# Where the statistics' tiny TensorE products sit: moved to other pairs of a conv-preact kernel

## The chip, the cores and the metric

The kernel runs on one core of a Trainium2 chip. The metric is the device time of one execution in microseconds (us), and the time of a kernel is the median of several runs. All arithmetic is float32.

## The reference, cut to what matters

The input x is 4 x 128 x 96 x 96 (batch, channels, rows, columns). Each batch is group-normalised over 32 groups of 4 channels, scanned in four directions by a small state-space block, fused and added to x:

```python
def _gn(v, G=32, eps=1e-5):
    g = v.reshape(B_, G, C_ // G, H_, W_)
    m = jnp.mean(g, axis=(2, 3, 4), keepdims=True)
    s = jnp.var(g, axis=(2, 3, 4), keepdims=True)
    return ((g - m) / jnp.sqrt(s + eps)).reshape(v.shape)
...
t = _grouped1x1(x, in_proj_w, in_proj_b, G)          # x is _gn(x) in one of four orders
u, gate = (t[:, :HID], t[:, HID:])
u = depthwise_conv5(silu(u))
...                                                  # s, a, bb, cc from u; scan along the sequence
u = u + _conv1x1(cc * hst + ssm_d[None, :, None] * s, ssm_out_w)
u = _grouped1x1(u * jax.nn.sigmoid(gate), mix_w, mix_b, G)
return _conv1x1(u, out_proj_w, out_proj_b)
...
x = x + fuse(four directions)
```

The kernel never normalises x. It scales the in_proj weights by 1/sqrt(variance) and puts the mean into the bias. For each batch it therefore needs, before that batch's first in_proj, the group means and variances, a scaled weight tile `wn` and a bias tile `bnorm`.

## The kernel before, in words

**Units and pairs.** There are 8 phases: for each of 4 batches one V phase (the two column directions) and one H phase (the two row directions). A phase has 24 pairs, so a batch has 48 pairs and the program 192 (`NU // 2`). `pair(t)` (L777) writes out the instructions of one pair by hand. The order of instructions on each engine is exactly the order of the code, because the whole body stands under a manual schedule. Below, "pair 38" means the pair with t % 48 = 38 of a batch: 0 to 23 are the V phase, 24 to 47 the H phase.

**What one pair issues on TensorE** (the lines are those of the profile; most products are recorded under the helper `mm`, L134): `conv` (`sil,band`), `accumulate` (`u,w_fin`, the output product of a unit six pairs back), `conv_less` (`sil,less`), `gate` (L491) and `out_of` (L497), and last `proj` (`u,main`, 32 loads and 32 matmuls). Pairs differ in three things:

- Pairs with t % 24 in 20 to 23 or 0 to 7 also compute in_proj (`x_in,wn` through L134) for the pair four ahead (`with_front`).
- Pairs with t % 24 in 6 to 17 compute gates (`gate`, L491). The other pairs read stored gates (`old`).
- So in the H half of a batch: pairs 24 to 29 have in_proj, 30 and 31 in_proj and gates, 32 to 41 gates alone, 42 and 43 neither, 44 to 47 in_proj.

TensorE uses three shapes of weight tile here: 128*32 and 64*32 (columns in four groups; `u,w_fin`, `u,main`, `sil,band`, the statistics, and `sil,less`), and 32*128 (gates and `out_of`). In_proj is 32*32.

**PSUM banks.** There are eight. Banks 0 to 3 take `out_of`; banks 0 and 1 also hold the running sum of the conv taps, which VectorE builds (L630). `PROJ` is (4, 5), `FRONT` is (7, 6, 2, 3). A pair takes its conv and proj banks and its accumulate banks `w` from `plan` (L125). In pairs 42 and 43 conv goes to banks 7 and 6, accumulate to 4 and 5, and proj to 4 and 5 at the end. With in_proj and fresh gates, the first gate goes to bank 6; with gates alone, to bank 4 (`GATE`, L123).

**The statistics of the next batch.** During the V phase VectorE takes chunk statistics of the next batch (`bn_stats`). At the end of pair 23 a generator `stats_finish(b + 1)` (L180) is made, and `stats_piece` (L818) advances it by one piece in every pair with t % 4 > 1. It has eight pieces:

1. `bn_aggr` on VectorE (`mv`).
2. Mean product: 4 matmuls `mv,gmean` (8 loads, a one-column right side) into bank `free[0]`; VectorE copies `mean` (L193), then `dev` (L195), `ex` (L197), `gm` (L199).
3. Variance product: 8 matmuls `ex,gmean` (16 loads); VectorE `var` (L207) and two integer steps on `inv`; GpSimd first Newton turn (4 tiny operations, L223 to L226).
4. and 5. Second and third Newton turn on GpSimd.
6. VectorE: two scalings that make `wn` (L230).
7. First bias product: 4 matmuls `gm,wn`; VectorE `bnorm` (L246), `shift` (L249), `spread` (L250).
8. Second bias product: 4 matmuls `spread,id`; VectorE `bnorm` (L255, L256).

Before the change the pieces fall in pairs 26, 27, 30, 31, 34, 35, 38, 39. Only three batches have a next batch: the last batch has none of these pieces.

**The bank of a tiny product** is `free[0]`. In pairs without in_proj, or with stored gates, it is `w[0]` (bank 7 in pair 27, bank 4 in pairs 38 and 39), straight after `accumulate` into `w[0]` and `w[1]`. In pairs 30 and 31 it is `w[1]`, bank 6, straight after `conv_less`.

**Around the end of a pair.** ScalarE copies finished conv sums out of PSUM into `us` (L609, or L611 for banks 6 and 7 in one instruction), copies `u` into the out_of banks (`under`, L505), and copies accumulate results to `ys` (L737). GpSimd adds `ys` to `acc` (L754). VectorE gates the finished unit (L577) and adds the taps of the next pair (L630); the last tap writes `us`, which `u,main` reads.

Of the kernel before, what the change touches and what calls it, by code (L numbers as in the profile page):

```python
# [63 lines left out]
NP = NS * R  # L64
# [3 lines left out]
def conv_preact_kernel(  # L68
# [53 lines left out]
    FRONT = (7, 6, 2, 3)  # L122
    GATE = {True: (6, 4, 5, 7), False: (4, 7, 6, 5)}  # L123

    def plan(with_front):  # L125

        return (PROJ, FRONT[:2]) if with_front else (FRONT[:2], PROJ)

    def bank(i):
        return psum[:, i, :]  # L130

    def mm(o, col, lhsT, rhs, start, stop):
        r = slice(32 * col, 32 * col + 32)
        nc.tensor.matmul(o[r, : rhs.shape[-1]], lhsT, rhs, start=start, stop=stop,  # L134
                         skip_group_check=True)
# [33 lines left out]
    stats, free = {}, [FRONT[1]]  # L169
# [92 lines left out]
    def fresh(step):  # L262

        return step * UB < NU and step % NS < NS // 2
# [11 lines left out]
    def mirror(n):  # L276

        return None if n % NP < NP // 2 else NP - 1 - n % NP
# [128 lines left out]
    def front_parts(i, banks, half=False):  # L407

        step, g = divmod(i, R)
        if step * UB >= NU:  # L410
            return
        st = step % NS
        if st == NS // 2:
            sils[step] = sils[step - 1]
            load_silu(step + 1, (g,))
        elif st == NS - 1 and g < 2:
            load_silu(step, (2 * g, 2 * g + 1))
        elif g == 0 and fresh(step):
            sils[step] = wk.tile([P, 2, 2, 4, N + 1], F32, tag="sil", name=f"sil_{step}")
        if fresh(step):  # L420
            yield from compute_front(step, g, banks, half)
        if st == 0:
            for j in range(2):
                edges(step, g, j, nc.gpsimd)
        after_front(step, g)
# [216 lines left out]
    def proj(i, banks, apart=False):  # L642

        step, p = units[i]["step"], units[i]["p"]
        if step not in scans:
            t0 = wk.tile([P, N, R], F32, tag="t0", name=f"t0_{step}")
            scans[step] = t0.rearrange("p n r -> p r n")
        ta = scans[step]
        tb = tbs[i] = wk.tile([P, N], F32, tag="t1", bufs=LAG + 1, name=f"t1_{units[i]['id']}")

        turns = [(e, j) for j in ((1, 0) if i else (0, 1)) for e in range(2)]
        apart = apart or not i
        for e, j in sorted(turns) if apart and i else turns:
            if i == 0 and (e, j) == (0, 0):
                first = front_parts(R, (5, 4, 2, 3), half=True)
                next(first)
                next(first)
                first_tap(2)
                for _ in first:
                    pass  # L660
            for c, cols in enumerate(((qb, qb, qa, qa), (qs, qs, qc, qc))[e]):
                first, end = (j == 0, j == 1) if apart else (j == 1, j == 0)
                mm(bank(banks[e]), c, w_proj[:, j, cols], us[i][:, c % 2, j, :], first, end)
        pa, pb = (bank(bk)[:, :N] for bk in banks)

        tm = tms[i] = wk.tile([P, N], F32, tag="tm", name=f"tm_{units[i]['id']}")
        nc.scalar.activation(tm, pa, AF.Tanh, bias=b_proj[:, 0:1])  # L667
        nc.scalar.copy(tb[0:64, :], pb[0:64, :])
        if i == NU - 2:
            nc.scalar.activation(  # L670
                ta[64:P, p, :], tm[64:P, :], AF.Identity, bias=mid[64:P, :], scale=HALF
            )
        nc.scalar.activation(tb[64:P, :], pb[64:P, :], AF.Tanh, bias=b_proj[64:P, 1:2])  # L673
        if i < NU - 2:
            nc.gpsimd.tensor_scalar(*decay(i))  # L675
        nc.gpsimd.tensor_mul(ta[0:64, p, :], tb[0:64, :], tm[0:64, :])  # L676

    def decay(i):

        a = scans[units[i]["step"]][64:P, units[i]["p"], :]  # L680
        return (a, tms[i][64:P, :], HALF, MID, ALU.mult, ALU.add)
# [5 lines left out]
    def first_tap(i):  # L687
        if i < NU:
            taps(i, range(1))
# [16 lines left out]
    def outputs(i, copy=nc.gpsimd.tensor_copy, engine=nc.gpsimd):  # L706
        ta, tb, p = scans[units[i]["step"]], tbs[i], units[i]["p"]
        engine.tensor_mul(ta[0:64, p, :], tb[64:P, :], ta[64:P, p, :])  # L708
        engine.tensor_add(tb[0:64, :], ta[0:64, p, :], tb[0:64, :])  # L709
        if copy:  # L710
            copy(tb[64:P, :], tb[0:64, :])  # L711
# [50 lines left out]
    later, soon = [], []  # L762
# [14 lines left out]
    def pair(t):  # L777
        i, k, bi = 2 * t, t % R, 2 * (t - LAG)
        back = bi >= 0
        old = back and mirror(bi // 2) is not None  # L780

        late = bi > 2 and (bi - 2) % (NU // B) == 0
        with_front = fresh((t + R) // R)
        final = (nc.vector, True) if t == NU // 2 - 1 else ()
        seed = old or back and not with_front

        ahead = old or back and not with_front
        banks, w = plan(with_front or not back)
        if not back:
            banks = head_banks(t)  # L790
        if back:
            front(t + R, FRONT)
        for n in soon:
            load_kept(n)
        soon.clear()
        if seed and not with_front:
            under(bi, 1)
        if t < NU // 2 - 2:
            send()

        if len(reload) == 4 and (k == 1 or late):
            for b, r in reload:
                nc.sync.dma_start(accf[:, r], xr[b, :, r])
            reload.clear()
        if t:
            new_u(i)
            taps(i, range(1, K))
            conv(i, banks)
        if t and not ahead:
            conv_less(i, banks)  # L810
        if not back and t:
            first_tap(i + 2)
            front(t + R, FRONT if banks == PROJ else (5, 4, 2, 3))
        recurrence(t)
        un = units[i]
        stats_chunks(t)

        def stats_piece():  # L818
            if later and k > 1:
                next(later[0], None)  # L820

        if not ahead:
            free[0] = w[1]
            stats_piece()
        if seed and with_front:
            for s in (1, 0):
                under(bi, s)
        for add in held:
            add()
        held.clear()  # L830
        if waiting:
            add = accumulate(waiting.pop(0), w[0], *final)
            if late:
                held.append(add)
            else:
                add()

        between = ahead and not old
        if between:
            conv_less(i, banks)  # L840
        if seed and not with_front:
            under(bi, 0)
        if ahead:
            accumulate(waiting.pop(0), w[1], *final)()
            free[0] = w[0]
            stats_piece()
            if not between:
                conv_less(i, banks)
        if old:
            scale_s(i - 2)  # L850
            for s in range(2):
                for j in range(2):
                    out_of(bi, s, j)
                load_gate(bi + s + UB)
        elif back:
            gates_and_out(bi, with_front)
        if back:
            for s in range(2):
                gating(bi, s)
        if un["order"] == "V" and un["b"] + 1 < B and un["st"] == NS - 1 and k == R - 1:  # L860
            later[:] = [stats_finish(un["b"] + 1)]
        if t + 2 < NU // 2:
            load_chunks(t + 2)
        if back:

            if k == 2 and t + 1 < NU // 2:
                soon.append(bi // 2 + 2)
            else:
                load_kept(bi // 2 + 2)
            if waiting:  # L870
                add = accumulate(waiting.pop(0), w[1])
                if late:
                    held.append(add)
                else:
                    add()
            first_tap(i + 2)
        if t == NU // 2 - 1:
            for s in range(2):
                under(bi + 2, s)
        if t == NU // 2 - 1:  # L880
            outputs(i - 8, None)
        proj(i, PROJ if back else banks, between)
        if not old and t > 0:
            scale_s(i - 2)
        if back:
            waiting.extend(units[bi : bi + 2])
        if t >= NU // 2 - 4:
            load_last(t)

        if bi > 0 and bi % (NU // B) == 0:  # L890
            send()
# [281 lines left out]
```

## Time and profile before

| what | value |
|---|---|
| median of 3 runs | 1819.84 us (1818.55 to 1820.01) |
| profiled execution, its own time | 1821.96 us |
| its span, first to last instruction | 1820.2 us |
| granted TensorE clock, mean | 0.998 |
| busy: PE, ACT, DVE, POOL | 98%, 86%, 80%, 78% |

How long single pairs take is read from the timeline of TensorE's weight loads: from the first load of one pair's `u,main` group to the first load of the next pair's. In us, for the pairs in question and for the same pairs of the last batch, which carry no statistics:

| pair of the batch | batch 0 | batch 1 | batch 2 | batch 3 |
|---|---|---|---|---|
| 26 | 9.265 | 9.264 | 9.264 | 9.264 |
| 27 | 9.822 | 9.816 | 9.816 | 9.264 |
| 28 | 9.328 | 9.384 | 9.384 | 9.327 |
| 30 | 9.954 | 9.954 | 9.955 | 9.828 |
| 31 | 10.178 | 10.181 | 10.180 | 10.182 |
| 34 | 9.110 | 9.110 | 9.110 | 9.110 |
| 35 | 9.111 | 9.111 | 9.111 | 9.111 |
| 38 | 9.690 | 9.689 | 9.690 | 9.109 |
| 39 | 9.624 | 9.621 | 9.622 | 9.111 |
| 42 | 8.410 | 8.407 | 8.408 | 8.408 |
| 43 | 8.251 | 8.251 | 8.250 | 8.251 |

A pair of one kind repeats to a few nanoseconds, so the rows can be compared directly. PE is TensorE's matmuls, PEld its weight loads, DVE VectorE, ACT ScalarE, POOL GpSimd. Matmul ends are modelled, so starts of loads are the firmer marks.

### The profile page before, as it was taken

What the parts mean: (1) busy time and instruction counts of PE and PEld (TensorE: products, weight loads), DVE (VectorE), ACT (ScalarE), POOL (GpSimd) and SP (SyncE); (2) the same over time, 40 slices, a digit from 0 to 9 for tenths busy, and PEclk for the clock granted to TensorE, in tenths of its full rate; (3) what the DMA queues carried; (4) which work ended last, traced back from release to release, by engine and by line L of the source; (5) the groups of instructions that cost most, each with busy time, mean ns of one, the idle gap of its engine ahead of it and who ended that gap; (6) DMA issues with size and microseconds to landing.
All of it is one profiled execution on the core that took longest, in us unless ns stands there. A gap on an engine that the chain in (4) does not pass through costs nothing.

```text
span 1820.2 us, 56934 instructions
## 1 busy us (share of the span) xinstructions
PE 1792.3 (98%) x24074; PEld 645.5 (35%) x24074; DVE 1454.6 (80%) x1462; ACT 1562.5 (86%) x2748; POOL 1428.2 (78%) x1475
## 2 busy tenths in 40 slices
PE   6999999999999999999999999999999999999998
PEld 3333333333333333333333333333333333333333
DVE  6888878877888888877778888887877788778885
ACT  4888888988988888888888888888888888888974
POOL 3587878778778888788877888887877888887785
PEclk9999999999999999999999999999999999999999
DMA  8555463444975465334696456453477644635434
GB/s 246 175 190 179 149 203 99 162 142 154 313 242 181 158 196 171 119 135 137 224 296 227 141 179 210 119 171 110 161 237 223 227 148 129 197 102 177 149 125 155
DMA packets 148047, 321.17 MB, mean 176 GB/s; under 512 B 14160, under 2 KB 115920, under 8 KB 147792
## 3 DMA queue, kind: packets, MB, share of 16 engines
q1 hardware_dynamic: 147648, 317.48, 54.2%
q8 instruction: 190, 3.11, 0.7%
q14 instruction: 65, 0.53, 0.1%
q10 hardware_dynamic: 144, 0.04, 0.0%
HBM read 185.21 MB, written 132.25 MB: 174 GB/s over the span
## 4 chain that ended last, share of the span: by engine, by line
PE 94%; ACT 2%; DVE 2%; DMA 1%; issue 0%; SPq 0%; POOL 0%; DVEq 0%; ACTq 0%; POOLq 0%
PE psum L134 81%; PE psum L497 8%; PE psum L491 5%; DMA xs<-in_xr 1%; ACT psum L505 1%; ACT sil L470 1%; DVE psum L630 1%; DMA acc<-in_xr 0%; DVE bn L298 0%; ACT u L611 0%; DVE u L577 0%; DVE u L630 0%; ACT psum L628 0%; DVE t L702 0%; SPq L296 0%
## 5 line engine op out<-in xcount | busy, mean ns | idle before, releaser
L630 DVE SCALAR_TENSOR_TENSOR psum<-sil,small,psum 128x768 f32<-128x768 f32 x576 | 589.0, 1023 | 28.8 <-ACT psum L628 3.4
L134 PE MATMUL psum<-u,w_fin 128*32 128x384 f32 x6176 | 553.1, 488 | 0.2 <-ACT t L673 0.2
L577 DVE SCALAR_TENSOR_TENSOR u<-gate,psum 128x768 f32<-128x768 f32 x376 | 349.8, 952 | 249.0 <-ACT gate L514 107.2
L134 PE MATMUL psum<-u,main 128*32 128x384 f32 x6144 | 534.9, 489 | 1.6 <-DVE u L630 1.5
L754 POOL TENSOR_TENSOR acc<-ys,acc 128x384 f32<-128x384 f32 x374 | 410.7, 1120 | 32.1 <-ACT ys L735 10.8
L708 POOL TENSOR_TENSOR t<-t,t 64x384 f32<-64x384 f32 x191 | 232.3, 1216 | 153.8 <-DVE t L702 70.2
L134 PEld LDWEIGHTS psum<-u,w_fin 128*32 128x32 f32 x6176 | 188.9, 110 | 322.4 <-issue 216.6
L134 PEld LDWEIGHTS psum<-u,main 128*32 128x32 f32 x6144 | 181.9, 109 | 328.4 <-issue 200.7
L505 ACT COPY psum<-u 128x768 f32<-128x768 f32 x352 | 276.7, 799 | 23.1 <-DVE u L630 11.3
L134 PE MATMUL psum<-sil,band 128*32 128x384 f32 x3072 | 285.2, 488 | 0.0
L675 POOL TENSOR_SCALAR t<-tm 64x384 f32<-64x384 f32 x191 | 177.2, 928 | 123.2 <-ACT tm L667 104.2
L709 POOL TENSOR_TENSOR t<-t,t 64x384 f32<-64x384 f32 x191 | 246.8, 1292 | 15.0
L497 PE MATMUL psum<-t,main 32*128 32x384 f32 x1536 | 242.1, 514 | 3.3 <-ACT psum L505 2.6
L628 ACT ACTIVATE psum<-sil,small 128x768 f32<-128x768 f32 x191 | 173.2, 907 | 61.1 <-DVE u L577 52.8
L514 ACT ACTIVATE gate<-psum,bnorm 128x384 f32<-128x384 f32 x384 | 192.1, 582 | 30.1 <-PE psum L491 28.6
L676 POOL TENSOR_TENSOR t<-t,tm 64x384 f32<-64x384 f32 x192 | 195.1, 1016 | 15.3
L630 DVE SCALAR_TENSOR_TENSOR u<-sil,small,psum 128x768 f32<-128x768 f32 x192 | 194.9, 1015 | 7.8
L470 ACT ACTIVATE sil<-psum,bnorm 128x385 f32<-128x385 f32 x384 | 192.1, 585 | 3.7 <-PE psum L134 1.5
L134 PE MATMUL psum<-sil,less 64*32 64x384 f32 x3072 | 168.1, 495 | 0.0
L491 PE MATMUL psum<-x_in,wn 32*128 32x384 f32 x768 | 157.4, 526 | 3.0 <-DVE shift L249 1.4
L711 POOL COPY t<-t 64x384 f32<-64x384 f32 x188 | 141.2, 751 | 15.5 <-PE psum L134 3.6
L134 PEld LDWEIGHTS psum<-sil,band 128*32 128x32 f32 x3072 | 90.3, 109 | 169.6 <-issue 94.4
(102 smaller groups left out, 1484.3 us busy)
## 6 DMA issues: line engine op xcount, KB each, us to landing
sil<-sil SPq DMA_DIRECT2D x128, 770.0 KB, 6.8
kept<-gate SPq DMA_DIRECT2D x80, 768.0 KB, 3.7
gate<-kept SPq DMA_DIRECT2D x76, 768.0 KB, 5.1
x_in<-in_xs SPq DMA_DIRECT2D x192, 96.2 KB, 2.5
out<-acc SPq DMA_DIRECT2D x48, 384.0 KB, 8.0
acc<-in_xr SPq DMA_DIRECT2D x39, 384.0 KB, 6.9
xs<-in_xr SPq DMA_DIRECT2D x72, 192.0 KB, 5.5
x_in<-in_xs SPq DMA_DIRECT2D x46, 192.5 KB, 3.5
```

Of the source, the lines that this page charges most:

```text
L134: nc.tensor.matmul(o[r, : rhs.shape[-1]], lhsT, rhs, start=start, stop=stop, skip_group_check=True)
L470: nc.scalar.activation(sils[step][:, s, j, g, :], bank(bk)[:, : N + 1], AF.Silu, bias=bn[:, 1:2] if j else bn[:, 4 + g : 5 + g],)
L491: nc.tensor.matmul(bank(to)[:, :N], stats[un["b"]][0][r, s, :], x_in[s][r, q, off : off + N], start=True, stop=True)
L497: nc.tensor.matmul(bank(SSM + 2 * s + j)[:, :N], w_so[r, bass.ts(j, P)], z[r, :], start=bi not in seeded, stop=True, skip_group_check=True)
L505: nc.scalar.copy(psum[:, SSM + 2 * s : SSM + 2 * s + 2, :N], us[bi][:, s])
L514: nc.scalar.activation(gv[:, s, j, :], bank(to[2 * s + j])[:, :N], AF.Tanh, bias=bn[:, 2 + j : 3 + j], scale=0.5,)
L577: nc.vector.scalar_tensor_tensor(v, g, 1.0, pz, ALU.add, ALU.mult)
L630: nc.vector.scalar_tensor_tensor(us[i][:, :, 1, :] if k == K - 1 else part, src, w_tap[:, k : k + 1], part, ALU.mult, ALU.add,)
L676: nc.gpsimd.tensor_mul(ta[0:64, p, :], tb[0:64, :], tm[0:64, :])
L708: engine.tensor_mul(ta[0:64, p, :], tb[64:P, :], ta[64:P, p, :])
L709: engine.tensor_add(tb[0:64, :], ta[0:64, p, :], tb[0:64, :])
L754: adder.tensor_add(part, y, part)
```

## The change

`stats_piece` gets a flag and a place. Pairs 27 and 39 no longer advance the generator. In pairs 42 to 47 (`ending`: stored gates, second half of the H phase) the usual call does nothing, and a second call stands after `out_of`, the gating and the loads, just ahead of `proj`, with bank 7 (`FRONT[0]`) as the product's bank. The eight pieces fall in pairs 26, 30, 31, 34, 35, 38, 42, 43. So the mean product is in pair 30 and the variance product in pair 31, both in the place where the variance product of pair 30 was; the Newton turns are in 31, 34 and 35; `wn` is made in 38; and the two bias products are in pairs 42 and 43, between `out_of` and `u,main`. The first batch's statistics, at the start of the program, and all other instructions keep their order.

```diff
@@ -815,8 +815,10 @@
         un = units[i]
         stats_chunks(t)
 
-        def stats_piece():
-            if later and k > 1:
+        ending = old and t % (2 * NP) > NP + NP // 2
+
+        def stats_piece(at_end=False):
+            if later and k > 1 and at_end == ending and t % (2 * NP) not in (27, 39):
                 next(later[0], None)
 
         if not ahead:
@@ -879,6 +881,9 @@
                 under(bi + 2, s)
         if t == NU // 2 - 1:
             outputs(i - 8, None)
+        if ending:
+            free[0] = FRONT[0]
+            stats_piece(True)
         proj(i, PROJ if back else banks, between)
         if not old and t > 0:
             scale_s(i - 2)
```

## The prediction

> **What bounds the kernel now.** I read the page first, then who waited for whom on TensorE, then the timeline around each tiny product.
>
> ```profile
> span 1820.2 us, 56934 instructions
> PE 1792.3 (98%) x24074; PEld 645.5 (35%) x24074; DVE 1454.6 (80%) x1462; ACT 1562.5 (86%) x2748; POOL 1428.2 (78%) x1475
> ...
> PE 94%; ACT 2%; DVE 2%; DMA 1%; issue 0%; SPq 0%; POOL 0%; DVEq 0%; ACTq 0%; POOLq 0%
> ```
>
> TensorE is the bound everywhere: 98% busy, and 94% of the chain that ended last. So an edit is worth what it does to the distance between TensorE's loads. Who waited on PE names the products at once:
>
> ```profile
> PE psum L491 <- DVE shift L249: 1.4, 3, 0.5
> PE psum L491 <- DVE bnorm L255: 1.2, 3, 0.4
> PE psum L134 <- ACT ys L737: 0.9, 3, 0.3
> ```
>
> Each is 3 times, once per batch that has a next one. But an idle time of PE is not the cost; the pair's length is. Loads of `u,main`, pair 38 of batch 0 and of batch 3 (no statistics):
>
> ```profile
> 362.76 0.16 PEld L134 LDWEIGHTS psum<-u,main 128*32 128x32 f32 x8 [0.57 <-ACT gate L514]
> 372.45 0.16 PEld L134 LDWEIGHTS psum<-u,main 128*32 128x32 f32 x8 [0.62 <-ACT gate L514]
> ...
> 1693.06 0.16 PEld L134 LDWEIGHTS psum<-u,main 128*32 128x32 f32 x8 [0.57 <-ACT gate L514]
> 1702.17 0.16 PEld L134 LDWEIGHTS psum<-u,main 128*32 128x32 f32 x8 [0.57 <-ACT gate L514]
> ```
>
> 9.69 against 9.11: the first bias product costs 0.58 us. The last batch is a control for every pair, and the table of pair lengths above gives the rest. The end of pair 38 shows why:
>
> ```profile
> 369.53 0.13 PEld L134 LDWEIGHTS psum<-u,w_fin 128*32 128x32 f32 x4 [0.19 <-issue]
> 369.85 0.13 PEld L134 LDWEIGHTS psum<-gm,wn 128*32 128x32 f32 x4 [0.19 <-ACT u L611]
> ...
> 370.66 0.15 DVE L249 COPY shift<-psum 128x1 f32<-128x1 f32 x1
> 370.76 1.18 POOL L709 TENSOR_TENSOR t<-t,t 64x384 f32<-64x384 f32 x1
> 370.85 1.12 DVE L250 TENSOR_SCALAR spread<-gmask,shift 128x4 f32<-128x4 f32 x1
> 370.87 0.19 PEld L491 LDWEIGHTS psum<-x_in,wn 32*128 32x128 f32 x2 [0.56 <-DVE shift L249]
> ```
>
> The next gate writes the product's bank 4, so it waits for VectorE's two reads: a round trip. Note too that `spread`, a 4-column operation, takes 1.12 us and ends at 371.97, just after POOL's L709 (371.94): such VectorE operations wait here for the GpSimd operation under way.
>
> **Removed, by pair, summed over the three batches** (table, against batch 3). Mean product in 27: 0.558 + 0.552 + 0.552 = 1.66; it waited for ScalarE's `ys` copy of bank 7. Its echo in pair 28 (VectorE late through `dev` and `ex`): 0.00 + 0.06 + 0.06 = 0.12. Variance product in 30: 3 x 0.126 = 0.38. Bias products: 38, 0.581 + 0.580 + 0.581 = 1.74; 39, 0.513 + 0.510 + 0.511 = 1.53. In all 5.43 us.
>
> **Mean product into pair 30: 0.19.** It takes the place of the variance product, whose 16 loads passed before `w_fin` in 0.12 us:
>
> ```profile
> 293.48 0.22 PEld L134 LDWEIGHTS psum<-ex,gmean 128*32 128x32 f32 x16 [0.62 <-ACT sil L470]
> 293.59 0.17 PEld L134 LDWEIGHTS psum<-u,w_fin 128*32 128x32 f32 x8
> ```
>
> Half the loads, so 0.063 a batch. Its bank 6 is written next by the first gate at 295.03; VectorE's `mean` would end near 294.05 (`var` before ended 294.08), so it is read in time. `dev`, `ex`, `gm` come ahead of L576, which started 296.68: `dev` released by POOL's L676 (ends 294.44), `ex` by L708 (295.73), `gm` right behind at about 295.9. Covered by 0.8 us. If `gm` had to wait for POOL's L709 (296.99), VectorE would be 0.4 us late.
>
> **Variance product into pair 31: 0.38.** Same place, 3 x 0.126. `var` must now wait for the last tap, which in pair 31 ends 304.82; so it ends about 305.0, and the first gate, at 305.18 plus 0.12, finds bank 6 read with 0.25 us to spare. If the VectorE delay above came true, that gate would wait some 0.15 us.
>
> **Newton turns and `wn`: nothing.** The pairs that already held a turn or `wn`, 34 and 35, are as long as in batch 3 (9.110, 9.111). In 38 the two `wn` operations lie between the last tap and the gating, 3.5 us in which VectorE waits for gates. Only 35 gets a turn that it did not have: it holds up GpSimd by about 1.0 us, as in 34 before, unnoticed there.
>
> **Bias products into 42 and 43: 1.35.** No other row shows a product there. Below stands what it meets in pair 42:
>
> ```profile
> 408.00 0.80 ACT L611 COPY u<-psum 128x768 f32<-128x768 f32 x1
> ...
> 408.70 0.16 PEld L134 LDWEIGHTS psum<-u,main 128*32 128x32 f32 x8 [0.55 <-issue]
> ```
>
> Its bank 7 is one that L611 still copies, until 408.81. `u,main` does not wait for that, as it begins with the half that VectorE makes. The product must: start at 408.86 (in pair 27 the load came 0.05 after the copy), 0.06 for its loads, then `u,main` at 408.92 instead of 408.70: 0.22. In pair 43 `conv_less` is 0.22 later, L611 follows it by 0.98 as before (415.29 to 416.27) and lasts 0.80, so product at 417.34 and `u,main` at 417.40 instead of 416.95: 0.45 for both, 1.35 for three batches. Lower bound 0.12 a batch (only loads, as in 30; not below nothing, since TensorE only gets more to do), upper bound with the tap chain late, among the rivals.
>
> The second thing there is VectorE. `bnorm`, `shift`, `spread` stand after the gating (ends 410.70) and ahead of the taps (L630, 410.81). Behind these queue the last tap (ends 415.00), `under` (415.04), `ys`, L611, and `out_of` and now the product behind those. POOL is in an add until about 411.1, where `spread` gets its turn: taps 0.3 late, L611 ready at the same 416.49 that `conv_less` sets. So I take it as covered, with no spare. In 43 the two `bnorm` steps delay the taps by 0.4 or less, no more than TensorE's own delay.
>
> A rule that speaks against the change: the Trainium skill, "TensorEngine Tiling (Array Packing)", Key Properties, says that changing the tiling mode drains TensorE, while another tile of the same mode does not. By it the products in 27 and 38 stand beside groups of their own shape, add no drain, and removing them saves only their loads; the sum would be near nothing. The rows (0.55 to 0.58 a piece) show a bank wait instead, and I go by them.
>
> **Sum.** 5.43 - 0.19 - 0.38 - 1.35 = 3.51 us saved. On the profiled execution: 1821.96 (span 1820.2 and 1.8 around it) to 1818.5. That execution is 2.1 above the median, so the median goes from 1819.84 to 1816.3, or -0.19%. A measurement of this kernel can tell about 0.2%, 3.64 us, from no change: the forecast lies almost on that line.
>
> **Rivals.**
>
> - *The ends of 42 and 43 are nearly free*, 0.12 a batch: 5.43 - 0.57 - 0.36 = 4.5 saved, 1815.3. For: L611 ended only 0.11 after the first `u,main` load, and 0.55 us of idle loads precede it. Against: the product cannot write the bank before that copy ends. 15%.
> - *A gate in 31 waits for `var`*: 0.15 x 3 given back, 1816.8. For: 0.25 us to spare only. 13%.
> - *`spread` in 42 misses its turn* and waits for POOL's second add (ends 412.08): taps 1.3 late, `under` ends at 417.2, L611 at 418.3, `u,main` about 1.4 late instead of 0.45, 1.0 more a batch: 1819.3. For: the 1.12 of pair 38. Against: the first add is under way when it arrives. 10%.
> - *Slower*: in the same place `spread` is passed over again and again, behind POOL's next L675 and L676 (to 414.19) as well. Taps 3.4 late go one for one through `under` and L611 to `u,main`: 3.5 a batch against 1.62 gained elsewhere, 1825.5. It decides from a delay of about 1.5 us on. Against: no small VectorE operation of this trace waited for more than the one POOL operation under way (1.16 at most). 5%.
> - That the products do not move is excluded by the built order of instructions: each stands where the change says, and no other row moves.
>
> **How the numbers follow.** Main case 57%, within 0.6 us of 1816.3, about half of it beyond the 3.64: 0.29 faster, 0.28 same. First rival 0.15 faster; second and third 0.23 same; slower 0.04 and 0.01 same. So 0.44, 0.52, 0.04. The range goes from the first rival, less half of the 1.3 us by which the lowest run lies under the median, 1814.6, to 1818.6, which takes in the second rival and part of the third, and leaves out the fourth.
>
> **What would show it.** Pair 27 at 9.26, 28 at 9.33, 38 and 39 at 9.11; 30 at 9.89, 31 at 10.31; 42 at 8.63 and 43 at 8.48. In the waits of PE, L249 and L255 are gone, and `gm,wn` and `spread,id` wait for L611. A pair 43 over 9.2 means the tap chain; a 31 over 10.4, the gate behind `var`. Wrong altogether if pairs outside these change.

## The result and the profile after

| | before | after |
|---|---|---|
| median of 17 runs | 1820.12 us (1818.34 to 1823.31) | 1816.32 us (1814.80 to 1824.61) |
| profiled execution, its own time | 1821.96 us | 1816.83 us |
| its span | 1820.2 us | 1815.0 us |

The ratio is 0.9982, with a 95% interval of 0.9975 to 0.9990. So the kernel is faster, by slightly less than the 0.2% that the forecast named as its line; the interval lies on both sides of that line but not over 1. The two medians differ by 3.80 us; the ratio alone would give about 3.3.

The page of the changed kernel, span, busy time and the chain that ended last:

```profile
span 1815.0 us, 56931 instructions
PE 1792.2 (99%) x24074; PEld 644.7 (36%) x24074; DVE 1444.8 (80%) x1462; ACT 1563.1 (86%) x2748; POOL 1428.1 (79%) x1475
...
PE 95%; DVE 2%; ACT 1%; DMA 1%; issue 0%; SPq 0%; DVEq 0%
```

TensorE's busy time is the same, 1792.2 against 1792.3 us: nothing was computed less. The span lost waits. In the list of who waited for whom on TensorE's matmuls (us in total, times, longest) the three rows of before are gone. The one statistics operation left is that of the start-up (`mv`), which stood there before too, with 1.0:

```profile
PE psum L997 <- DMA acc<-in_xr: 11.7, 1, 11.7
PE psum L497 <- ACT psum L505: 2.6, 2, 2.0
PE psum L134 <- DVE u L630: 0.8, 2, 0.4
PE psum L134 <- DVE u L577: 0.6, 1, 0.6
PE psum L491 <- ACT u L609: 0.4, 1, 0.4
PE psum L134 <- ACT t L673: 0.2, 1, 0.2
PE psum L134 <- DVE mv L188: 0.2, 1, 0.2
```

Pair 38, from one `u,main` to the next in the timeline of weight loads, is now 9.11, as in a batch without statistics:

```profile
361.10 0.16 PEld L134 LDWEIGHTS psum<-u,main 128*32 128x32 f32 x8 [0.57 <-ACT gate L514]
...
370.21 0.16 PEld L134 LDWEIGHTS psum<-u,main 128*32 128x32 f32 x8 [0.57 <-ACT gate L514]
```

The end of pair 42, where the first bias product now stands:

```profile
405.25 0.80 ACT L611 COPY u<-psum 128x768 f32<-128x768 f32 x1
...
406.10 0.16 PEld L134 LDWEIGHTS psum<-gm,wn 128*32 128x32 f32 x8 [0.70 <-ACT u L611]
...
406.16 0.16 PEld L134 LDWEIGHTS psum<-u,main 128*32 128x32 f32 x8
...
407.34 1.98 POOL L754 TENSOR_TENSOR acc<-ys,acc 128x384 f32<-128x384 f32 x2
...
408.11 0.27 DVE L250 TENSOR_SCALAR spread<-gmask,shift 128x4 f32<-128x4 f32 x1
...
408.30 1.01 DVE L630 SCALAR_TENSOR_TENSOR psum<-sil,small,psum 128x768 f32<-128x768 f32 x1
```

L611 ends at 406.05, the product's loads follow at 406.10, `u,main` 0.06 later. `spread` ends at 408.38, just after GpSimd's first add (408.35), and the taps (L630) stand behind it on VectorE.

Two executions must be compared with care here. The profiles differ by 5.1 us and the medians by 3.8. Up to the `u,main` of pair 8 of batch 0, before any moved instruction, the profiled execution of before took 95.61 us and that of after 94.47; over all twelve profiled executions of this study that stretch took 94.5 to 102.6 us, though none of the kernels differs there. It is the start-up, and the differences lie in pairs 0, 3 and 4. The two longest, 102.6 (`c_unread`) and 100.4 (`i_27bank6`), have a granted clock of 0.5 for some 10 and 7 us of it; the other ten are 94.5 to 97.5. From there to the last `u,main` the two took 1684.21 and 1680.45: **3.76 us less**. That stretch is used below, since in it a pair of one kind repeats to a few nanoseconds.

### The profile page after: what moved, and what is told of

It reads as the page before. It is cut to its first block, busy times and chain, and to the rows that moved or that the text cites. A ratio compares the mean times of both kernels' runs of the same rounds, so it can differ in the third digit from the quotient of the medians.

```text
span 1815.0 us, 56931 instructions
## 1 busy us (share of the span) xinstructions
PE 1792.2 (99%) x24074; PEld 644.7 (36%) x24074; DVE 1444.8 (80%) x1462; ACT 1563.1 (86%) x2748; POOL 1428.1 (79%) x1475
## 4 chain that ended last, share of the span: by engine, by line
PE 95%; DVE 2%; ACT 1%; DMA 1%; issue 0%; SPq 0%; DVEq 0%
PE psum L134 82%; PE psum L497 8%; PE psum L491 5%; DVE psum L630 1%; DMA xs<-in_xr 1%; DMA acc<-in_xr 0%; DVE u L577 0%; DVE bn L298 0%; DVE u L630 0%; ACT sil L470 0%; ACT psum L505 0%; ACT psum L628 0%; SPq L296 0%; ACT u L611 0%; PE psum L1004 0%
## 5 line engine op out<-in xcount | busy, mean ns | idle before, releaser
L630 DVE SCALAR_TENSOR_TENSOR psum<-sil,small,psum 128x768 f32<-128x768 f32 x576 | 589.0, 1023 | 28.1 <-ACT psum L628 3.4
L577 DVE SCALAR_TENSOR_TENSOR u<-gate,psum 128x768 f32<-128x768 f32 x376 | 349.8, 953 | 275.1 <-ACT u L609 119.2
L505 ACT COPY psum<-u 128x768 f32<-128x768 f32 x352 | 276.7, 799 | 23.3 <-DVE u L630 11.4
L628 ACT ACTIVATE psum<-sil,small 128x768 f32<-128x768 f32 x191 | 173.2, 907 | 57.3 <-DVE u L577 49.5
L630 DVE SCALAR_TENSOR_TENSOR u<-sil,small,psum 128x768 f32<-128x768 f32 x192 | 194.9, 1015 | 7.8
L711 POOL COPY t<-t 64x384 f32<-64x384 f32 x188 | 137.0, 729 | 15.5 <-DVE t L709 3.6
```

The costliest lines, as they stand in the source:

```text
L505: nc.scalar.copy(psum[:, SSM + 2 * s : SSM + 2 * s + 2, :N], us[bi][:, s])
L577: nc.vector.scalar_tensor_tensor(v, g, 1.0, pz, ALU.add, ALU.mult)
L630: nc.vector.scalar_tensor_tensor(us[i][:, :, 1, :] if k == K - 1 else part, src, w_tap[:, k : k + 1], part, ALU.mult, ALU.add,)
```

## The experiments

Lengths of pairs are read as in the table above, in us, for batches 0 to 2 (one number where they agree to 0.02). "Steady" is the stretch just described, against 1684.21 before.

| kernel | 27 | 28 | 30 | 31 | 38 | 39 | 42 | 43 | 44 | steady, change |
|---|---|---|---|---|---|---|---|---|---|---|
| before | 9.82 | 9.33 to 9.38 | 9.95 | 10.18 | 9.69 | 9.62 | 8.41 | 8.25 | 9.33 | |
| after | 9.26 | 9.33 | 9.89 | 10.31 | 9.11 | 9.11 | 8.62 | 8.49 | 9.27 | -3.76 |
| `a_means` | 9.26 | 9.33 | 9.89 | 10.30 | 9.69 | 9.62 | 8.41 | 8.25 | 9.33 | -1.65 |
| `b_bias` | 9.81 | 9.34 to 9.36 | 9.95 | 10.18 | 9.11 | 9.11 | 8.62 | 8.49 | 9.27 | -2.17 |
| `c_unread` | 9.82 | 9.33 to 9.42 | 9.95 | 10.18 | 9.15 | 9.15 | 8.41 | 8.25 | 9.33 | -3.03 |
| `d_spread2` | 9.26 | 9.33 | 9.89 | 10.30 | 9.11 | 9.11 | 8.62 | 9.35 | 9.27 | -1.14 |
| `e_early` | 9.26 | 9.33 | 9.89 | 10.31 | 9.17 | 9.17 | 8.41 | 8.25 | 9.33 | -4.54 |
| `f_bank4` | 9.26 | 9.33 | 9.89 | 10.30 | 9.11 | 9.11 | 10.60 | 10.40, 11.84 | 9.26 | +9.34 |
| `g_middle` | 9.26 | 9.33 | 9.89 | 10.31 | 9.11 | 9.11 | 8.41 | 8.37 to 8.41 | 9.33 | -4.50 |
| `h_27late` | 9.44 | 9.73 to 9.78 | 9.95 | 10.18 | 9.69 | 9.62 | 8.41 | 8.25 | 9.33 | +0.04 |
| `i_27bank6` | 10.19 | 9.33 | 9.96 | 10.18 | 9.69 | 9.62 | 8.41 | 8.25 | 9.33 | +1.00 |

The kernels `after_again`, `g_middle` and `e_early` were run 12, 7 and 12 times, beside 25 runs of before. The other seven ran once each, and their times decide nothing: `c_unread` took 1825.27 us, 4.4 more than before beside it, with 3.03 less in the steady stretch and the long start-up of 102.6 us. For these seven the lengths of pairs are the evidence.

**Each part alone.** The means and variances:

```diff
-            if later and k > 1:
+            if later and (k > 1 or t % (2 * NP) == 33) and t % (2 * NP) != 27:
```

> One part alone: mean product in pair 30 and variance product in pair 31, bias products in 38 and 39 as before (the second Newton turn takes pair 33, which holds no TensorE work of the statistics). If the parts are independent, pair 27 is 9.26, 28 is 9.33, 30 is 9.89, 31 is 10.31, 38 stays 9.69 and 39 stays 9.62, 42 and 43 stay 8.41 and 8.25: about 0.54 us a batch less than before, 1.6 us in all. If the two parts help each other, as a rival has it (VectorE's earlier delays decide the round trip in 38), 38 and 39 move by more than 0.05.

And the bias products, as the change has them but with the pieces in 26, 27, 30, 31, 34, 35, 42, 43:

```diff
-            ... and t % (2 * NP) not in (27, 39):
+            ... and t % (2 * NP) not in (38, 39):
```

> The other part alone: bias products at the ends of pairs 42 and 43, mean and variance in 27 and 30 as before. Independent parts: 27 is 9.82, 30 is 9.95, 31 is 10.18, 38 and 39 are 9.11, 42 is 8.62, 43 is 8.49, 44 is 9.27: about 0.69 us a batch less than before, 2.1 us in all.

-1.65 and -2.17 us: together -3.82, against -3.76 for both. The parts are independent to within 0.06 us, and the bias products bring more than half.

**Is the price in 38 and 39 the round trip or the loads?** The kernel before, its products unchanged, with VectorE reading SBUF instead of bank 4:

```diff
-            nc.vector.tensor_sub(bn[:, 0:4], b_in[:, 0:4], pb[:, 0:4])
+            nc.vector.tensor_copy(bn[:, 0:4], b_in[:, 0:4])
...
-            nc.vector.tensor_copy(shift, pb[:, 0:1])
+            nc.vector.tensor_copy(shift, gm4[:, 0:1])
...
-            nc.vector.tensor_sub(bn[:, 4:8], b_in[:, 4:8], pq[:, 0:4])
+            nc.vector.tensor_copy(bn[:, 4:8], b_in[:, 4:8])
```

> The kernel before, bias products issued in 38 and 39 as before, but VectorE does not read them: it fills bnorm and shift from SBUF instead, so the bias of batches 1 to 3 is not computed. Round trip theory (the gate's wait for VectorE's reads is the cost): 38 and 39 fall to about 9.2. Theory of the loads (8 loads of a tiny product behind running matmuls cost two steps of 0.30 us whoever reads the result): 38 and 39 stay at 9.5 to 9.65, and VectorE's read explains 0.1 us at most.

Both pairs are 9.147. The product's own loads cost 0.037 us, the round trip 0.54 in 38 and 0.47 in 39. The timeline of pair 38 in this kernel shows how little is left when nobody reads:

```profile
376.59 0.13 PEld L134 LDWEIGHTS psum<-u,w_fin 128*32 128x32 f32 x4 [0.19 <-issue]
376.91 0.13 PEld L134 LDWEIGHTS psum<-gm,wn 128*32 128x32 f32 x4 [0.19 <-ACT u L611]
377.24 0.13 PEld L134 LDWEIGHTS psum<-gm,wn 128*32 128x32 f32 x4 [0.19 <-issue]
377.38 0.19 PEld L491 LDWEIGHTS psum<-x_in,wn 32*128 32x128 f32 x2
```

The loads come in waves of four; two waves of long matmuls stand 0.32 us apart. Pair 37 of the kernel before has no product, and there the gate's load, of another shape, follows straight on the accumulate:

```profile
360.42 0.13 PEld L134 LDWEIGHTS psum<-u,w_fin 128*32 128x32 f32 x4 [0.19 <-issue]
361.18 0.19 PEld L491 LDWEIGHTS psum<-x_in,wn 32*128 32x128 f32 x2 [0.62 <-ACT u L611]
```

From the start of the accumulate's last wave to the gate's load it is 0.76 us without a product, and 0.79 with the product's two waves in between (376.59 to 377.38). The gate's load comes only 0.14 after the product's last wave. So the tiny product passes almost wholly in the time that goes by at this place anyway.

**The bank and its copy, in pair 27.** The kernel before, once with the mean product in bank 6, once moved behind `conv_less`:

```diff
-            free[0] = w[0]                                      # i_27bank6
+            free[0] = w[1] if t % (2 * NP) == 27 else w[0]
...
-            stats_piece()                                       # h_27late
+            if t % (2 * NP) != 27:
+                stats_piece()
             if not between:
                 conv_less(i, banks)
+            if t % (2 * NP) == 27:
+                stats_piece()
```

> The kernel before with the mean product of pair 27 in bank 6 instead of 7, at the same place. ScalarE copies bank 6 second, 0.38 us after bank 7. Wait for the copy: pair 27 grows from 9.82 to about 10.2. Price of the product or of the drain itself: 27 stays at 9.82.

10.19: as forecast, 0.37 more, the distance between the starts of the two copies. The wait for ScalarE's copy sets the price.

> The kernel before with one move inside pair 27: the mean product stands after conv_less instead of ahead of it, same bank 7, same pair. ScalarE's copy of that bank has then ended. If the wait for the copy is the price (the prediction), pair 27 falls from 9.82 to about 9.33 although the pair is the same; pair 28 keeps its echo of up to 0.06. If the kind of pair is what counts (products are cheap only beside gates), 27 stays near 9.8.

Half a miss. Pair 27 falls to 9.44, so the copy's wait is gone (and 0.11 is paid on top of the loads, between two groups of other shapes). But pair 28 grows by 0.34 to 0.41, and nothing is gained in sum. The timeline at the start of pair 28 shows the way:

```profile
271.83 1.80 DVE L577 SCALAR_TENSOR_TENSOR u<-gate,psum 128x768 f32<-128x768 f32 x2
...
272.81 0.91 ACT L628 ACTIVATE psum<-sil,small 128x768 f32<-128x768 f32 x1 [1.79 <-DVE u L577]
...
273.69 0.18 PEld L134 LDWEIGHTS psum<-x_in,wn 32*32 32x32 f32 x16 [0.28 <-DVE u L577]
...
274.60 0.58 ACT L673 ACTIVATE t<-psum,small 64x384 f32<-64x384 f32 x1
...
275.22 0.16 PEld L134 LDWEIGHTS psum<-sil,band 128*32 128x32 f32 x8 [0.57 <-ACT t L673]
```

`dev`, `ex` and `gm` stand ahead of VectorE's gating (L577). The second half of in_proj's loads waits for the gating, which ends at 273.63; from in_proj to `sil,band` it takes 1.27 instead of the 0.94 of an undisturbed pair 28. ScalarE's first tap (L628) waits for the gating too, the copies of the proj banks (L667, L668, L673) stand behind L628 in ScalarE's order, and the second half of `conv` waits for the last of them, L673. That last wait is the echo that pair 28 showed before the change (in batch 1 there, `sil,band` at 717.04, 0.55 of idle time, ended by L673), here at a larger dose.

The earlier product could not help VectorE, because `ex` ends with GpSimd's second add in both kernels: at 271.78 and 271.76 here, at 269.89 and 269.86 before. So the gating begins 10.75 us after the `u,main` of pair 26 here and 10.71 before, and what TensorE gains in pair 27 it waits for in pair 28. So a cheap place needs two things: a bank that is ready, and spare time on VectorE behind the product. Pair 30 has both.

**Bank against place, in 42 and 43.**

```diff
-            free[0] = FRONT[0]
+            free[0] = PROJ[0]
```

> The changed kernel with the bias products of 42 and 43 in bank 4 instead of bank 7. The product then need not wait for ScalarE's copy, but u,main writes bank 4 next and has to wait for VectorE, which reads the product only after its gating. By the bank rule 42 and 43 grow to about 10.5 each, some 4 us a batch and 12 us in all over the changed kernel. If only the place counts and not the bank, they stay at 8.5 to 8.6.

10.60 and 10.40, but 11.84 for pair 43 in one batch. There the granted clock was 0.69 from 857 to 862 us, where it was 1.00 in the other two batches, and the waves of `u,main` stood 0.64 us apart instead of 0.32. In all it is 13.1 us over the changed kernel, or 11.7 without these 1.4, so the 12 of the forecast. The waits of TensorE name the two reads that now hold up `u,main`:

```profile
PE psum L134 <- DVE shift L249: 5.8, 3, 1.9
PE psum L134 <- DVE bnorm L255: 5.7, 3, 1.9
```

**VectorE's spare time behind `spread`.**

```diff
             nc.vector.tensor_scalar_mul(spread, gmask, shift)
+            nc.vector.tensor_mul(spread, spread, gmask)
```

> The changed kernel with one more VectorE step behind spread in pair 42 (spread times the mask again, which changes no value), so that VectorE has to wait for GpSimd's second add as well. If the tap chain behind it has no spare, as the prediction says, the taps start 1.0 to 1.3 us later and pair 43 grows from 8.49 to about 9.5: 3 us in all. If there is spare time of more than 1 us between the last tap and the end of the pair, pair 43 stays at 8.49.

Pair 43 grows by 0.87, a little less than forecast. The timeline of VectorE, where L251 is the added step and L631 the first tap:

```profile
410.13 0.28 DVE L250 TENSOR_SCALAR spread<-gmask,shift 128x4 f32<-128x4 f32 x1
410.45 0.92 DVE L251 TENSOR_TENSOR spread<-spread,gmask 128x4 f32<-128x4 f32 x1
411.29 1.01 DVE L631 SCALAR_TENSOR_TENSOR psum<-sil,small,psum 128x768 f32<-128x768 f32 x1
```

GpSimd's two adds run here from 409.38 to 411.36; the first step gets its turn between them, the second only behind both. The taps begin 1.0 us later than without it, and 0.87 of that reaches TensorE: there is next to no spare time, and this one more step costs 2.6 us in all, more than the 2.17 that the bias products bring.

**The changed kernel again, and two better places.** The change itself once more, beside the next two:

> The changed kernel itself, beside the next ones on one chip. Ratio to before 0.998, about 1816.3 us; the lengths of pairs 27 to 44 as in its first profile, within 0.01 us.

The ratio is 0.9979 (0.9969 to 0.9988), with 1817.95 us, where before took 1822.57: the runs of that series are slower and wider for both, so the 1816.3 was not met and the ratio was. All pairs from 27 to 44 agree with the first profile to 0.01 us.

The bias products between the two halves of `u,main`:

```diff
...
+            if n == 2 and middle:
+                middle()
...
-        proj(i, PROJ if back else banks, between)
+        proj(i, PROJ if back else banks, between, (lambda: stats_piece(True)) if ending else None)
```

> The changed kernel with the bias products of 42 and 43 put between the two halves of u,main, still into bank 7, when ScalarE's copy of that bank has ended. If the wait for that copy is what the changed kernel pays there, the product costs 0.04 us, as the unread products did in a running stream: 42 is 8.45, 43 is 8.29, and the time falls by 0.3 to 0.4 us a batch, about 1.1 us to 1815.2. If the price is the tiny product itself ahead of u,main, 42 and 43 stay within 0.05 of 8.62 and 8.49.

42 is 8.41 (the first product lies behind the mark that ends it), 43 is 8.39 on average, and 44 stays at 9.33 with the second product in it. Of the 0.14 that the first product adds to pair 43, 0.06 are its loads. The rest arises at `out_of` and `u,main`: ScalarE's copy into the out_of banks (L505) waits for VectorE's last tap and starts 0.25 later in the pair than before, which agrees with taps that are still late. The second product's loads cost 0.06 as well, for in_proj of pair 44 begins 2.78 after the `u,main` ahead of it instead of 2.72; the pair is no longer for it because a wait of 0.06 inside in_proj is gone, as in the changed kernel (see the missed term below). So the price of 0.04 a product and the 8.29 for pair 43 were missed by 0.02 and 0.1, and the saving is 0.74 us over the change, not 1.1. Ratio to before 0.9972 (0.9961 to 0.9982), median 1817.36: in the times it cannot be told from the change.

And the bias products in 38 and 39, ahead of the second accumulate:

```diff
-            if later and k > 1:
+            if later and (k > 1 or t % (2 * NP) == 33) and t % (2 * NP) != 27:
...
         if ahead:
+            free[0] = w[0]
+            early = between and t % (2 * NP) > 36
+            if early:
+                stats_piece()
             accumulate(waiting.pop(0), w[1], *final)()
-            free[0] = w[0]
-            stats_piece()
+            if not early:
+                stats_piece()
```

> Means and variances as in the changed kernel; the bias products back in 38 and 39, into bank 4, but ahead of the second accumulate (right after conv_less), so that VectorE has read bank 4 long before the gate writes it. Round trip theory: 38 and 39 are 9.15 to 9.20, 42 to 44 as in the kernel before, about 0.3 us a batch less than the changed kernel, near 1815.4. If a change of weight shape ahead of the product costs anything of its own, 38 and 39 are above 9.3.

9.174 in both: 0.064 a product, the same as that of the mean product in pair 30, in the very pairs that cost 0.58 and 0.51. The timeline of pair 38:

```profile
368.37 0.16 PEld L134 LDWEIGHTS psum<-gm,wn 128*32 128x32 f32 x8 [0.62 <-ACT ys L735]
368.43 0.16 PEld L134 LDWEIGHTS psum<-u,w_fin 128*32 128x32 f32 x8
...
368.83 0.15 DVE L249 COPY shift<-psum 128x1 f32<-128x1 f32 x1
...
369.86 0.19 PEld L491 LDWEIGHTS psum<-x_in,wn 32*128 32x128 f32 x2 [0.62 <-issue]
```

VectorE has read the bank by 368.98, almost 0.9 us before the gate wants it; the accumulate's matmuls fill the round trip. In the steady stretch this is the shortest kernel, 4.54 us under before and 0.78 under the change. In the times, 0.9984 (0.9974 to 0.9993) with a median of 1818.89 where the changed kernel had 1817.95, it cannot be told from the changed kernel: 0.8 us is 0.04%, and the interval is 0.19% wide.

## Why the prediction was right, point by point

The forecast was 1816.3 us, 3.51 saved. 1816.32 was measured, 3.80 under a median of before that had itself moved from 1819.84 (3 runs) to 1820.12 (17 runs). The steady stretch lost 3.76. By its own line of 0.2% the forecast gave "same" 0.52 and "faster" 0.44, and the result lies on the line: by the ratio just on the first side, by the medians (3.80 against 3.64 us) just on the second. The terms can be checked one by one, summed over three batches:

| step | forecast | measured in the trace |
|---|---|---|
| mean product out of 27, echo in 28 | -1.66, -0.12 | -1.66, -0.11 |
| pair 30, mean for variance | -0.19 | -0.19 |
| variance product in 31 | +0.38 | +0.38 |
| bias products out of 38 and 39 | -1.74, -1.53 | -1.74, -1.54 |
| bias products into 42 and 43 | +1.35 | +0.64, +0.71 |
| pairs 32 and 44 | 0 | -0.06, -0.17 |
| sum (rounded; the steady stretch lost 3.76) | -3.51 | -3.74 |

- *The control.* The last batch carries no statistics, so the removed terms were read, not estimated. They had to come out.
- *The waits taken over.* The product in 42 waits for L611 and in 43 again, 0.21 and 0.23 a pair, from the end of a copy, 0.05 to the load, 0.06 for the loads. `spread` got its turn at the end of GpSimd's first add, as expected.
- *The missed term* is pair 44. Before, its `conv` began 0.94 after in_proj's first load; after, 0.88. The timeline names ScalarE's L668 at this load in both kernels, but that copy ends at the same place in both, 3.33 us after `u,main`, 0.33 and 0.27 ahead of the load. The difference lies among in_proj's own loads. TensorE's queue holds instructions there that only wait for a semaphore (EVENT_SEMAPHORE): two before (`before`, 419.6 to 420.7 us), one after (`after`, 417.3 to 418.3):

```profile
L134 PEldq EVENT_SEMAPHORE  x2: 51/51/51, 419.7 to 419.9; - x2
...
L134 PEldq EVENT_SEMAPHORE  x1: 51/51/51, 417.5 to 417.5; - x1
```

The one that is gone stood behind the fourth load; the page counts three instructions fewer, 56931 for 56934, one a batch. In all twelve traces it is 0.94 or more from in_proj's first load to `conv` in those of pairs 24, 28 and 44 that have such an early one, and 0.88 in those that have none, as in pairs 25 and 29. So 0.06 a batch of the price is given back by one wait instruction less. Why the new order needs one less was not followed up. Pair 32 is 0.02 shorter in `a_means` too, so that part belongs to the means and variances; its cause stays open.
- *The rivals.* The free end of 42 and 43 was refuted by the lengths; `f_bank4` shows that the place alone does not make it cheap. The gate in 31 did not wait: 10.306 is the forecast 10.31. A `spread` that misses its turn did not happen, but `d_spread2` shows the mechanism and its price, 0.87 a batch where 1.0 was worked out. Nothing came near the slower one.
- *The rule on changing the tiling mode* (the Trainium skill, "TensorEngine Tiling (Array Packing)", Key Properties) would have put the gain near nothing. `c_unread` measures a product that follows a group of its own shape, 0.037 us, so for the tiny products themselves the trace agrees with it; the half microsecond was the bank's round trip, of which that section says nothing.

The median's agreement to 0.02 us is luck: the interval of the ratio is 0.15% wide, some 2.7 us, and before's shift by 0.28 hid the missed term of about the same size. The agreement of the single terms is not.

## What to carry to other kernels

When one engine is the bound and its order is fixed, a tiny operation costs what it waits for, and what waits for its result's buffer, not what it computes: place it where its bank was freed some time ago and where other work lies between it and the bank's next writer. Before moving work to another stage, try it a few instructions earlier in the same one; here that cost 0.06 us in a place that had cost 0.58. And look for an iteration that does not carry the work: it is a control that prices every wait to a few nanoseconds, long before the run times can tell.

## What the hardware showed that was not expected

- A load group of another shape started 0.76 us after the last wave of a 384-column group (0.32 between waves of one shape), but only 0.14 us after a wave of a 4-column product that itself followed such a group. A tiny product at that point, of the shape of the group ahead of it, cost 0.037 us. Between two groups that both had another shape (`h_27late`, pair 27) the mean product cost 0.17.
- A wait instruction (51 ns) behind the fourth of in_proj's 32 loads on TensorE's queue went with 0.06 us more for the group in every trace; one near the end of the group did not.
- A 4-column VectorE operation from SBUF to SBUF (`spread`) took 0.27 to 1.21 us, depending on the GpSimd operation under way (in pair 38 before it ended 0.03 us after that one, 371.97 and 371.94); it got its turn between two adds that stood back to back, and a second one, which reads the first one's result, ended only with the next add (0.92).
- Between executions, the start-up to pair 8 varied by 3 us (94.5 to 97.5), and by 8 where the granted clock fell to 0.5 for some us of it, while the remaining 1680 us repeated to a few hundredths between two executions of the changed kernel (1680.45 and 1680.49).
